# Router logits carried as eight extra columns of a graph layer's products and edge sums

## The chip, the core and the metric

The kernel runs on one NeuronCore of a Trainium2 chip. The metric is the device time of one execution in microseconds (us). All arithmetic is float32.

## What is computed

A graph layer is followed by a mixture of eight experts with two chosen per node. There are 6250 nodes with 256 features and 100000 edges, sorted by destination.

```python
x = x + gnn(layernorm(x))          # agg = segment_sum(h[src], dst) / max(deg, 1)
                                   # concat([h, agg]) @ W.T + b,  W is 256 x 512
x = x + ffn(layernorm(x))
# ffn: layernorm again, * gamma + beta = xn
# logits = xn @ Wr + br            (8 experts)
# top 2, softmax over them = w
# y = sum over e of w[e] * (gelu(xn @ W1[e] + b1[e]) @ W2[e] + b2[e])
```

## The kernel before

**Lead.** W is split into halves. `center_weights` subtracts the column means from each half, which gives `gc`, so that a product with the raw x is the layer norm's product up to the factor 1/deviation. The 49 tiles of 128 nodes are taken in blocks of four (`TB`). For each block `z_block` multiplies the transposed x (`x_t`, loaded in that form) with the second half of `gc` (line 198), ScalarE scales by the reciprocal deviation and writes `zt` (line 226), and SP stores it to `z_d` in DRAM (line 229). Between the products of a block, VectorE computes the statistics of the next one (`z_statistics`, lines 162 and 163) and then its reciprocal deviations (`z_deviations`: a variance, a square root on ScalarE, a reciprocal and a Newton step of four instructions). Loads run four blocks ahead. From the fourth block on one further step is done after every second tile (`steps`, line 393): constants, the turning of the edge lists with a cast to integers (line 274), the first row of every window, and four checks that the destinations do not descend (`compare`, lines 284 and 287).

**Edge stage.** The edges are cut into 56 windows of 14 tiles of 128 edges. For every tile POOL issues an indirect load of 128 rows of `z_d` into one of 16 buffers `xg` (line 527). TensorE multiplies them with a one-hot matrix `hot` of their destinations and accumulates in PSUM (`pS`, line 544); a 257th column of ones counts the degree. A row that two windows share is handed on through DRAM. Beside this `u_stages` computes u = x + b + first half of the product, two node tiles at a time, on the first 50 edge tiles, into `u_d`. At the end of a window x1 = u + sums/degree (`window_x1`, line 581), and its statistics are taken.

**Routing.** After four windows (a group) the second layer norm gives `xn` (line 453). `turn` transposes it on TensorE (line 465) and ScalarE evicts it with gamma and beta (line 466); `route` multiplies it with Wr (line 476), and VectorE computes the ranks (lines 482 to 497), ScalarE the exponentials, VectorE the weights and the slots. `sort_tokens` (line 627) moves the rows to their experts' places by a one-hot product, `copy_runs` (line 742) gathers them by register offsets.

**Experts.** A chunk is 4 or 8 windows (sizes 4, 8, 8, 8, 8, 8, 4, 4, 4). The expert products (lines 758, 773, and for overfull experts 790 to 808) are tasks that are spread over the edge tiles by a rate that comes from a deadline; their rows go to `y_d`. Later POOL gathers each node's two rows (line 856), VectorE adds them (line 863), and SP stores the result.

**What sets the order.** The program order on every engine is written out by hand. The class `Steps` says after how many edge tiles a step of the routing follows a window's end, for example `turn` after 15 and `route` after 20, or 10 and 13 in the last two chunks. After the last edge tile the same counter runs on without gathers.

Of the kernel before, what the change touches and what calls it, by code (L numbers as in the profile page):

```python
# [8 lines left out]
F32 = mybir.dt.float32  # L9
# [8 lines left out]
P = 128  # L18
# [13 lines left out]
def gnn_ffn_kernel(ctx: ExitStack, tc: tile.TileContext, x, x_cols, src, dst, gw_t, gb, gamma, beta,  # L32
# [41 lines left out]
    DA = D + 1  # L74
# [22 lines left out]
    z_d = dram.tile([HR, D], F32, name="z_d")  # L97
    u_d = dram.tile([HR, D], F32, name="u_d")
# [23 lines left out]
    gc = u_pool.tile([P, 2 * KD, D], F32, name="gc", bufs=1)  # L122
    early_pools = ctx.enter_context(ExitStack())
    early = early_pools.enter_context(tc.tile_pool(name="early", bufs=2, side="right"))
    gw_sb = early.tile([P, 2 * KD, D], F32, name="gw_sb", bufs=1)
    for h in (1, 0):
        nc.scalar.dma_start(gw_sb[:, h * KD:(h + 1) * KD, :],
                            gw_t[h * D:(h + 1) * D, :].rearrange("(k p) o -> p k o", p=P))
    order = ctx.enter_context(ExitStack())
# [9 lines left out]
    def constants():  # L139
        nc.vector.tensor_scalar(before, ej, 0.0, None, op0=ALU.is_lt)  # L140
        nc.vector.tensor_copy(cols, coli)
        nc.vector.tensor_copy(lane, lanei)
        nc.vector.tensor_scalar(upper, col, lane, None, op0=ALU.is_gt)
# [40 lines left out]

    def center_weights(h):
        pc = ps.tile([P, D], F32, name="pm")
        for k in range(KD):
            nc.tensor.matmul(pc, ones, gw_sb[:, h * KD + k, :], start=(k == 0), stop=(k == KD - 1))
        for k in range(KD):
            nc.vector.scalar_tensor_tensor(gc[:, h * KD + k, :], pc, -1.0 / D, gw_sb[:, h * KD + k, :],  # L190
                                           op0=ALU.mult, op1=ALU.add)

    def product(t0, n, k0):

        pz = ps.tile([P, 2, D], F32, name="ph")
        for i in range(n):
            for k in range(KD):
                nc.tensor.matmul(pz[:, i, :], x_t[:, t0 + i, k, :], gc[:, k0 + k, :],  # L198
                                 start=(k == 0), stop=(k == KD - 1))
        return pz  # L200

    def z_statistics(t0, some):
        n = min(TB, NT - t0)
        if 0 in some:
            mvs[t0] = small.tile([P, TB, 2], F32, name="mv")
        for i in some:
            if i < n:
                statistics(mvs[t0][:, i, :], xts[t0][:, i, :])

    def z_deviations(t0):  # L210
        n = min(TB, NT - t0)
        a = small.tile([P, TB], F32, name="var_eps")
        nc.vector.tensor_scalar(a[:, :n], mvs[t0][:, :n, 1], EPS, None, op0=ALU.add)
        rsqrt(rstd_x[:, t0:t0 + n], a, root(a, n, TB), n, TB)

    def z_block(t0, between):

        n = min(TB, NT - t0)
        after = t0 + TB
        zt = early.tile([P, TB, D], F32, name="zt", bufs=3)  # L220
        for i in range(0, n, 2):
            m = min(2, n - i)
            pz = product(t0 + i, m, KD)
            for j in range(m):
                t = t0 + i + j
                nc.scalar.activation(zt[:, i + j, :], pz[:, j, :], AF.Identity, scale=rstd_x[:, t:t + 1])
# [3 lines left out]
            if after in blocks:  # L230
                z_statistics(after, range(i, i + 2))
            if between:
                between.pop(0)()
        if after in blocks:
            z_deviations(after)
# [25 lines left out]
    def place_edges(parts, follow):  # L261
# [8 lines left out]
        def turn_edges(f, to, c0):  # L270
# [3 lines left out]
            nc.vector.tensor_copy(to.rearrange("p g c -> p c g")[:, c0:c0 + HC, :], pt)  # L274

        QE = EW // 4
        down = early.tile([W, QE], F32, name="down", bufs=1)

        def compare(i):

            at, n = i * QE, QE if i < 3 else QE - 1
            if i == 0:
                nc.vector.memset(wrong, 0.0)
            nc.vector.tensor_tensor(down[:, :n], fs[0][:, at + 1:at + 1 + n], fs[0][:, at:at + n], op=ALU.is_lt)
            if n < QE:
                nc.vector.tensor_tensor(down[:, n:], follow, fs[0][:, EW - 1:], op=ALU.is_lt)
            nc.vector.reduce_sum(wrong[:W, i:i + 1], down, axis=AX.X)
# [885 lines left out]
```

## Time and profile before

| | us |
|---|---|
| runs (median, lowest, highest of 3) | 1253.08, 1251.77, 1257.36 |
| profiled execution, its own time | 1255.72 |
| its span, first to last instruction | 1253.9 |
| mean granted TensorE clock | 0.948 |

In a line of the profile, L527 is line 527 of the kernel; the engine, the operation and the tiles follow, then the count, the busy time in us, the mean of one in ns, and the idle time of the engine before these instructions with what ended it. PE is TensorE's matmul and PEld its weight load, DVE is VectorE, ACT ScalarE, SPq the queue of SyncE. In the timeline a line starts with start and duration in us; instructions of one kind that follow each other are merged, and the brackets hold the idle time before and what ended it. A float32 matmul is two records.

### The profile page before, as it was taken

How to read it: one execution, taken by the hardware profiler on the slowest of the kernel's cores; microseconds unless marked ns; L12 is line 12 of the kernel's file. 1: busy time of each engine (PE TensorE's matmuls, PEld its weight loads, DVE VectorE, ACT ScalarE, POOL GpSimd, SP SyncE). 2: the span in 40 equal slices, each digit the busy share in tenths (PEclk: the TensorE clock that was granted, in tenths of full speed). 3: DMA queues.
4: the chain of work that ended last, by engine and by line, in shares of the span. 5: the costliest groups of instructions: out<-in, count | busy, mean ns of one | idle time of the engine just before them, and what ended most of it. 6: DMA issues, size and time to landing. Idle time of an engine off the chain costs nothing. (4 is left out here: it accounts for less than half of the span.)

```text
span 1253.9 us, 18359 instructions
## 1 busy us (share of the span) xinstructions
PE 1098.8 (88%) x5114; PEld 907.8 (72%) x5114; DVE 679.0 (54%) x2072; ACT 460.8 (37%) x1183; POOL 865.7 (69%) x911
## 2 busy tenths in 40 slices
PE   7798848687888999899998999899999899999872
PEld 6676736565656888688867887688867787877761
DVE  6765638353664448353754447354743647457541
ACT  3310011622074334733374334632374253533510
POOL 2047777777777777777777777777777777656652
PEclk9899988899898999899998999899999999999886
DMA  9879894554544555455554555555554565566663
GB/s 330 286 249 315 250 369 141 139 139 132 146 138 127 154 147 150 141 144 148 142 160 131 148 146 151 142 140 151 139 158 142 164 170 167 150 188 204 189 213 89
DMA packets 139585, 217.17 MB, mean 173 GB/s; under 512 B 23140, under 2 KB 106927, under 8 KB 139350
## 3 DMA queue, kind: packets, MB, share of 16 engines
q0 software_dynamic: 43104, 117.72, 35.2%
q1 hardware_dynamic: 89430, 89.31, 21.7%
q10 hardware_dynamic: 6944, 8.91, 2.1%
q8 instruction: 43, 0.70, 0.2%
q14 instruction: 64, 0.52, 0.1%
HBM read 162.32 MB, written 53.57 MB: 172 GB/s over the span
## 5 line engine op out<-in xcount | busy, mean ns | idle before, releaser
L527 POOL DMA_INDIRECT xg<-z_d,src_i x784 | 748.4, 955 | 292.6 <-issue 110.6
L544 PE MATMUL pS<-xg,hot 128*128 128x257 f32 x1568 | 428.8, 395 | 43.9 <-DMA xg<-z_d,src_i 29.9
L544 PEld LDWEIGHTS pS<-xg,hot 128*128 128x128 f32 x1568 | 295.0, 196 | 118.0 <-DMA xg<-z_d,src_i 51.5
L758 PE MATMUL ph<-xe,w_sb 128*128 128x256 f32 (+1 forms) x1152 | 223.7, 345 | 29.7 <-ACT xe L742 28.0
L758 PEld LDWEIGHTS ph<-xe,w_sb 128*128 128x128 f32 x1152 | 188.4, 199 | 50.8 <-ACT xe L742 30.4
L773 PE MATMUL py<-w_sb,hid 128*128 128x256 f32 x896 | 216.6, 387 | 7.1 <-DVE rows L777 7.1
L773 PEld LDWEIGHTS py<-w_sb,hid 128*128 128x128 f32 x896 | 172.3, 194 | 33.2 <-DVE rows L777 9.2
L765 ACT ACTIVATE hid<-ph,b_sb 128x256 f32<-128x256 f32 (+1 forms) x288 | 103.1, 426 | 232.5 <-PE ph L758 232.3
L742 ACT ACTIVATE xe<-xs x448 | 139.3, 311 | 60.1 <-ACT xe L742 36.1
L538 DVE TENSOR_TENSOR hot<-cols,rel 128x896 f32<-128x896 f32 x112 | 121.1, 1081 | 36.4 <-PE pS L544 32.4
L856 POOL DMA_INDIRECT xg<-y_d,rows_i x90 | 86.8, 965 | 64.5 <-issue 20.0
L198 PE MATMUL ph<-gc,x_t 128*128 128x256 f32 x392 | 100.8, 412 | 13.6 <-DVE u_t L351 10.5
L198 PEld LDWEIGHTS ph<-gc,x_t 128*128 128x128 f32 x392 | 80.1, 208 | 30.0 <-DVE u_t L351 12.1
L630 ACT ACTIVATE xs<-pm,beta_sb,gamma_sb 128x256 f32<-128x256 f32 x112 | 57.2, 561 | 109.7 <-PE pm L627 109.6
L550 DVE TENSOR_TENSOR pS<-pS,row 1x257 f32<-1x257 f32 x55 | 22.9, 417 | 116.1 <-PE pS L544 90.1
L777 DVE TENSOR_TENSOR rows<-py,b_sb 128x512 f32<-128x512 f32 x56 | 38.5, 688 | 84.5 <-PE py L773 84.5
L554 ACT ACTIVATE sums<-pS 128x257 f32<-128x257 f32 x56 | 21.5, 383 | 170.4 <-DMA xu<-x_dram 58.7
L627 PE MATMUL pm<-to,xn 128*128 128x256 f32 x224 | 59.2, 387 | 10.2 <-DVE rest L659 3.5
L863 DVE SCALAR_TENSOR_TENSOR xg<-xg,w,xg 128x256 f32<-128x256 f32 x90 | 42.8, 483 | 34.4 <-DMA xg<-x_d 22.0
L790 PE MATMUL ph<-w_sb,xe 128*128 x108 | 53.6, 621 | 4.3 <-DVE rows L794 3.3
L808 PE MATMUL py<-w_sb,hid 128*128 x216 | 53.6, 392 | 4.1 <-ACT hid L802 2.5
L627 PEld LDWEIGHTS pm<-to,xn 128*128 128x128 f32 x224 | 42.4, 192 | 19.5 <-issue 10.9
(172 smaller groups left out, 904.2 us busy)
## 6 DMA issues: line engine op xcount, KB each, us to landing
y_d<-rows SPq DMA_DIRECT2D x56, 256.0 KB
xg<-z_d,src_i POOLq DMA_INDIRECT x784, 2.9
w_sb<-w_dram ACTq DMA_DIRECT2D x16, 512.0 KB
x_d<-x SPq DMA_DIRECT2D x56, 128.0 KB
sums_d<-sums SPq DMA_DIRECT2D x55, 128.5 KB
x<-u_d SPq DMA_DIRECT2D x55, 128.0 KB
x_t<-x_cols_dram SPq DMA_DIRECT2D x12, 512.0 KB
xu<-x_dram SPq DMA_DIRECT2D x24, 256.0 KB
```

What stands on the lines that cost most here:

```text
L198: nc.tensor.matmul(pz[:, i, :], x_t[:, t0 + i, k, :], gc[:, k0 + k, :], start=(k == 0), stop=(k == KD - 1))
L527: nc.gpsimd.indirect_dma_start(out=xg[(g * C + c) % XG][:, :D], out_offset=None, in_=z_d[:, :], in_offset=bass.IndirectOffsetOnAxis(ap=src ...
L538: nc.vector.tensor_tensor(hot, col[:, None, :].to_broadcast([P, HC, P]), V.rel[:, c:c + HC, None].to_broadcast([P, HC, P]), op=ALU.is_equal)
L544: nc.tensor.matmul(V.pS, V.hot[c // HC][:, c % HC, :], xg[(V.g * C + c) % XG], start=(c == 0), stop=(c == C - 1))
L627: nc.tensor.matmul(px[:, k, :], G.xn[i][:, k * P:(k + 1) * P], G.one_hot[i], start=True, stop=True)
L630: nc.scalar.activation(xs[:, at:at + 2 * P], px[:, k, :], AF.Identity, bias=beta_sb[:, k:k + 1], scale=gamma_sb[:, k:k + 1])
L742: nc.scalar.activation(K.xe[:, :, bass.ds(v[2 * i], CAP)], src[:, :, bass.ds(src_at, CAP)], AF.Copy)
L758: nc.tensor.matmul(ph[:, i, a * S:(a + 1) * S], w1_sb[:, U.e + a, k, c * P:(c + 1) * P], K.xe[:, k, (U.e + a) * S:(U.e + a + 1) * S], star ...
L765: nc.scalar.activation(U.hid[:, c, a * S:(a + 1) * S], ph[:, i, a * S:(a + 1) * S], AF.Gelu, bias=b1_sb[:, U.e + a, c:c + 1])
L773: nc.tensor.matmul(U.py[:, h, :], U.hid[:, c, h * P:(h + 1) * P], w2_sb[:, U.e + h * UE // 2, c, :], start=(c == 0), stop=(c == KH - 1))
L790: nc.tensor.matmul(ph, K.xe[:, k, at:at + P], w1_sb[:, bass.ds(T.e, 1), k, :].rearrange("p a h -> p (a h)"), start=(k == 0), stop=(k == KD ...
L856: nc.gpsimd.indirect_dma_start(out=V.y2[r], out_offset=None, in_=y_d[K.index][:, :], in_offset=bass.IndirectOffsetOnAxis(ap=G.rows[:, r, i ...
```

## The change

The router's logits are linear in x1 up to mean, deviation and a constant. With wg = gamma * Wr and rc = wg less its column means, the logits are (x1 @ rc) / deviation + (beta @ Wr + br). So x1 @ rc is carried along. W.T @ rc is appended to each half of W.T as eight columns, `z_d`, `u_d`, the edge sums and x1 get 264 columns instead of 256 (the degree's column is then the 265th), and u's product gets eight more columns for x @ rc itself. The transposes, their evictions and the product with Wr are dropped from the routing; four small VectorE instructions per group, one per window, take their place, and the steps behind them move 5 or 7 edge tiles forward.

In the lead, the deviations are computed for groups of 4, 4, 8, 8, 8, 8, 8 and 1 tiles, ahead of the blocks; each node tile's product has a PSUM buffer of its own (two of `ph`, two of `pm`, each with one tile, instead of two of `ph` with two tiles); the casts of the edge lists and of `cols` go to ScalarE; the comparisons become subtractions on POOL with one maximum each on VectorE. The router's small products are added, as are loads of W in its own layout, of b by columns, and the loads of Wr, gamma, beta and br come first.

```diff
+    DZ = D + NX
+    DA = DZ + 1
-    z_d = dram.tile([HR, D], F32, name="z_d")
-    u_d = dram.tile([HR, D], F32, name="u_d")
+    z_d = dram.tile([HR, DZ], F32, name="z_d")
+    u_d = dram.tile([HR, DZ], F32, name="u_d")
...
+    nc.scalar.dma_start(wr_sb, wr.rearrange("(k p) e -> p k e", p=P))
+    nc.scalar.dma_start(gamma_sb, gamma)
     for h in (1, 0):
+        nc.scalar.dma_start(gw_rows[:, :, h * D:(h + 1) * D],
+                            gw[:, h * D:(h + 1) * D].rearrange("(k p) i -> p k i", p=P))
+        nc.scalar.dma_start(gw_sb[:, h * KD:(h + 1) * KD, :D],
                             gw_t[h * D:(h + 1) * D, :].rearrange("(k p) o -> p k o", p=P))
+    nc.scalar.dma_start(gb_p, gb_cols)
+    nc.scalar.dma_start(beta_sb, beta)
+    nc.scalar.dma_start(br_sb, bass.AP(tensor=br.tensor, offset=br.offset, ap=[[0, P], [1, NX]]))
...
+    def router_weights():
+        for k in range(KD):
+            nc.vector.tensor_scalar(wg[:, k, :], wr_sb[:, k, :], gamma_sb[:, k:k + 1], None, op0=ALU.mult)
+        for k in range(KD):
+            nc.tensor.matmul(pr, ones, wg[:, k, :], start=(k == 0), stop=(k == KD - 1))
+        for k in range(KD):
+            nc.vector.scalar_tensor_tensor(rc[:, k, :], pr, -1.0 / D, wg[:, k, :], op0=ALU.mult, op1=ALU.add)
+    def router_columns(h):
+        for i in range(KD):
+            for k in range(KD):
+                nc.tensor.matmul(pr[:, i, :], gw_rows[:, k, h * D + i * P:h * D + (i + 1) * P], rc[:, k, :],
+                                 start=(k == 0), stop=(k == KD - 1))
+        nc.vector.tensor_copy(gw_sb[:, h * KD:(h + 1) * KD, D:], pr)
...
+    def product(t, h):
+        n = DZ if h else DZ + NX
+        pz = ps.tile([P, n], F32, name=("ph", "pm")[t % 2])
+        for k in range(KD):
+            nc.tensor.matmul(pz, x_t[:, t, k, :], gc[:, h * KD + k, :n], start=(k == 0), stop=(k == KD - 1))
...
+    def z_deviations(S):
+        a = small.tile([P, 2 * TB], F32, name="var_eps")
+        nc.vector.tensor_scalar(a[:, :S.n], S.mv[:, :S.n, 1], EPS, None, op0=ALU.add)
+        rsqrt(rstd_x[:, S.first:S.first + S.n], a, root(a, S.n, 2 * TB), S.n, 2 * TB)
...
-            nc.vector.tensor_copy(to.rearrange("p g c -> p c g")[:, c0:c0 + HC, :], pt)
+            nc.scalar.activation(to.rearrange("p g c -> p c g")[:, c0:c0 + HC, :], pt, AF.Copy)
...
+            nc.gpsimd.tensor_tensor(down[:, :n], fs[0][:, at:at + n], fs[0][:, at + 1:at + 1 + n], op=ALU.subtract)
-            nc.vector.tensor_tensor(down[:, :n], fs[0][:, at + 1:at + 1 + n], fs[0][:, at:at + n], op=ALU.is_lt)
-            nc.vector.reduce_sum(wrong[:W, i:i + 1], down, axis=AX.X)
+            nc.vector.reduce_max(wrong[:W, i:i + 1], down, axis=AX.X)
...
+                pu = product(t, 0)
+                nc.vector.tensor_tensor(B.ut[:, i, D:], pu[:, DZ:], gb_r, op=ALU.add)
+                nc.vector.scalar_tensor_tensor(B.ut[:, i, :], pu[:, :DZ], rstd_x[:, t:t + 1], B.ut[:, i, :],
...
-    def turn(G, k):
-        pt = ps.tile([P, TG, P], F32, name="pm")
-        for i in range(G.n):
-            nc.tensor.transpose(pt[:, i, :], G.xn[i][:, k * P:(k + 1) * P], ident)
-        nc.scalar.activation(G.xn_t[:, k, :G.n, :], pt[:, :G.n, :], AF.Identity,
-                             bias=beta_sb[:, k:k + 1], scale=gamma_sb[:, k:k + 1])
+    def logits(G):
+        for i in range(n):
+            nc.vector.scalar_tensor_tensor(lg[:, i, :], G.x1[i][:, D:], G.scale[:, i:i + 1], router_b,
+                                           op0=ALU.mult, op1=ALU.add)
     def route(G, work):
-                nc.tensor.matmul(pl[:, i, :], G.xn_t[:, k, i, :], wr_sb[:, k, :],
-                                 start=(k == 0), stop=(k == KD - 1))
...
-            out=xg[(g * C + c) % XG][:, :D], out_offset=None, in_=z_d[:, :],
+            out=xg[(g * C + c) % XG][:, :DZ], out_offset=None, in_=z_d[:, :],
...
-                self.x1, self.var, self.roots, self.norms, self.turn = 2, 4, 5, 7, 10
-                self.route, self.exps, self.weigh, self.choices, self.count = 13, 15, 16, 17, 19
-                self.hot, self.sort, self.each, self.tiles, self.copied, self.pace = 22, 25, 1, 22, 28, 1
+                self.x1, self.var, self.roots, self.norms = 2, 4, 5, 7
+                self.route, self.exps, self.weigh, self.choices, self.count = 8, 10, 11, 12, 14
+                self.hot, self.sort, self.each, self.tiles, self.copied, self.pace = 17, 20, 1, 17, 23, 1
```

## The prediction

> **What bounds the kernel now.** I read the page's busy shares first, then the gather's group, then the POOL timeline piece by piece, because the shares alone (PE 88%, POOL 69%) point to the wrong engine.
>
> ```profile
> PE 1098.8 (88%) x5114; PEld 907.8 (72%) x5114; DVE 679.0 (54%) x2072; ACT 460.8 (37%) x1183; POOL 865.7 (69%) x911
> L527 POOL DMA_INDIRECT xg<-z_d,src_i x784 | 748.4, 955 | 292.6 <-issue 110.6
> ...
> L476 PEld LDWEIGHTS pm<-wr_sb,xn_t 128*128 128x128 f32 x224 | 28.6, 200 | 7.0 <-ACT xn_t L466 6.3
> L465 PEld LDWEIGHTS pm<-ident,xn 128*128 128x128 f32 x112 | 15.0, 149 | 4.5 <-DVE xn L453 1.2 <-DVE pS L550 0.6
> ```
>
> A gather occupies POOL for 0.946 us (the median), and 0.30 us pass before the next one whatever the reason given. From the first gather to the last, the timeline shows that beat almost unbroken:
>
> ```profile
> 74.99 1.15 POOL L527 DMA_INDIRECT xg<-z_d,src_i  x1 [52.59 <-DVE rel L535]
> ...
> 1084.86 0.94 POOL L527 DMA_INDIRECT xg<-z_d,src_i  x1 [0.30 <-issue]
> ...
> 1087.36 0.95 POOL L527 DMA_INDIRECT xg<-z_d,src_i  x1 [0.30 <-issue]
> ```
>
> Between 75.0 and 1087.4 POOL issues 784 node gathers and some 20 row gathers in 1012.4 us, 1.25 us each; gaps above 0.33 us add only about 1.3 us (0.44, 0.91 and 0.99), instructions longer than 1 us about 7 us. So the span is three pieces: a lead of 75.0 us, an edge stage of 1012.4 us set by POOL, and a tail of 166.5 us.
>
> The lead, by windows (the columns after the stretch are PE, PEld, DVE, ACT, POOL busy, granted clock, DMA share, GB/s):
>
> ```profile
> 20.00:40.00 20.00, 17.18 (x93) 13.46 (x91) 17.32 (x73) 8.06 (x22) 1.89 (x2) 1.00 1.07 392
> 40.00:60.00 20.00, 16.15 (x58) 12.97 (x58) 15.14 (x67) 5.43 (x16) 0.00 (x0) 0.83 0.75 264
> L162 DVE BATCH_NORM_STATS2 st<-xt 128x6 f32<-128x256 f32 x49 | 19.7, 402 | 0.0
> ```
>
> VectorE is full but for its waits on the root (10.8 us in all), and it never waits for a load (idle 0.0 before the statistics). DMA is saturated too from 20 to 45 us, but four blocks ahead of the compute. The tail, by the timeline:
>
> ```profile
> 1112.30 0.60 PE L544 MATMUL pS<-xg,hot 128*128 128x257 f32 x2
> ...
> 1130.96 1.97 PEld L476 LDWEIGHTS pm<-wr_sb,xn_t 128*128 128x128 f32 x16
> ...
> 1178.61 7.33 PEld L758 LDWEIGHTS ph<-xe,w_sb 128*128 128x128 f32 x64
> ...
> 1233.72 0.94 POOL L856 DMA_INDIRECT xg<-y_d,rows_i  x1 [17.24 <-DMA y_d<-rows]
> ```
>
> The last gather goes out at 1087.4, yet PE adds its edges only at 1112.3: PE lags by nearly the ring of 16. The last chunk is routed until 1178.6, its experts run to 1231, and POOL waits 17.24 us for their rows.
>
> **The lead.** Removed from VectorE: 5 of 13 deviation chains (8 groups remain: 4, 4, five of 8, and 1), each 1.4 us from the variance to the last Newton step including the wait for the root, so 7.0 us; four index casts of 0.81 and one of `cols` of 0.42, 3.7 us, which go to ScalarE; four comparisons of 0.59, 2.4 us, which go to POOL before its first gather, when it idles 52.6 us. Added: two products, two subtractions and three small copies for the router, the bias tiles and two copies of rc, about twelve instructions of 0.13 to 0.3 us, 2 us. VectorE's total goes from 26 (49 statistics at 0.53 a pair) + 18.2 + 6.1 + about 7 of other steps = 57 us, which is what the 60.9 us between the first zt (11.40) and the last (72.30) show, to 26 + 11.2 + 7 + 2 = 46.
>
> PE: a weight load and its matmul are one record each; a record at 256 columns comes every 0.216 us. Eight more columns are taken in proportion, 0.223. The z products are 196 such records, 43.7 us, plus turns, centring, router columns and biases, about 6 us; some 3.6 us of it fit into PSUM before the first zt. So PE too needs about 46 us. ScalarE gets five casts of some 0.5 us (the nearest row is zt, 0.47 for 256 elements) on 24 us busy in 75: covered by its waits; behind a cast that waits for its transposes stand the next zt, for well under a microsecond. The comparisons on POOL have a price on VectorE: while POOL cast an index tile, one Newton product took 1.44 us instead of 0.16 (start 18.79). Four such hits would be 5 us, none 0; most VectorE instructions beside that cast kept their time, so I count 1, inside the margin below.
>
> The new wait is at the front. wr, gamma and gw's rows now precede gw_t on ACT's queue: three issues of 0.48 us and 256 KB at 395 GB/s (0.66 us) put its landing from 4.3 to 6.4 us. PE's centring, all z products behind it and VectorE's first statistics behind rc wait for that, so the first zt comes at about 13.5 instead of 11.4.
>
> 13.5 + 46.4 = 60, plus 2.7 from the last zt to the first gather (72.3 to 75.0) is 63, a gain of 12, if nothing interferes. DMA: 21.7 MB moved in the lead, now 0.5 MB of gw rows and 0.2 MB of wider z more, 22.4 MB at 395 GB/s is 57 us, plus about 3 at the start and 4 for the last block: 64. The five small loads that used to run at 86 to 91 us join the saturated stretch too; each has 128 to 256 tiny pieces, and I allow 1 to 3 us. ACT issues seven loads more, before any of its work; SP loses four at 86 to 90 us and otherwise keeps its order. With two limits at 63 to 66 and none of the overlap perfect, I take 67.5: **-7.5 us**, ends 0 and -12.
>
> **A rule against the wider rows.** In 300 to 900 us the DMA view gives the gathers' queue
>
> ```profile
> q0 software_dynamic: 22957, 62.73, 40.0%
> ```
>
> for 479 gathers: 48 packets each and 0.50 us of all 16 engines (40% of 600 us / 479). The Trainium skill, "DMA: Bandwidth & Descriptors", section "How a descriptor splits into AXI transactions", says that reads go in pieces of 256 B from aligned addresses. A 1024-byte row is 4 pieces; one of 1056 bytes starting at a multiple of 32 touches always 5, with 36.5 beats on average against 32. By that rule a gather takes 0.57 to 0.63 us of the engines (estimate), the stage's DMA share goes from 0.53 to about 0.6, and nothing is lost in the edge stage: 1.25 us of POOL covers it. In the lead, z writes of 6.4 MB (16 us at 395 GB/s) would take 2 to 4 us more, and the gain there would be -4. By the row above (bytes alone, +3%) it is -7.5; I keep that, since no compute waits for a load there today, and hold the 3.5 for the range. From 80 to 120 us, where DMA is at 1.00 and 0.93, gathers land later; the ring of 16 (20 us) covers that, and without it up to 5 us would be lost.
>
> **The edge stage.** The gather moves 264 elements instead of 256. No row shows POOL at another width: every gather of this kernel has 1024-byte rows. If POOL's 0.946 us goes by rows (128 in both), it costs nothing; if by bytes, 3.1% is 29.6 ns, times 784 is 23.2 us. It may not fall, as no row or index goes. The equal 946 ns from z_d, u_d and y_d fits work per row, so I take 0, and both ends count below. PE: 1568 records grow by 2.6% (6.7 ns each from 0.216), +10.5 us, and u's 196 records by 16 columns, +2.6; removed are the transposes and logits, 336 records. In the tail one group's take 0.58 + 0.58 + 1.97 us, about 3.1, so 14 groups 44. The net -31 us of PE lies under POOL and is worth nothing before 1087, as are 22 us of ScalarE (xn_t, 28 x 0.78) and VectorE's +9 (u's bias columns, 49 x 0.19) and +8 (56 logits of 0.19 against 14 sums). Stage: **0 us**.
>
> **The tail.** PE reached the ring's full depth only after 950 us. In its last 130 tiles two groups are routed, -6.4, and the edges add 1.7; but routing ends 5 or 7 tiles earlier, so the experts too start earlier and put about 4 us before the last edges (chunk 7's 42 us of tasks over 56 tiles, five tiles more). PE at 1112.3 comes forward only by about 1. Then from 1112.3 to 1178.6, 66 us, PE has 54 us of work: 128 records of L758 (15), 64 of L773 (14), L808 and L790 (15), sort (4), the router (3.1), the rest 3. Of that go 3.1 and the 4 already done; and the last group's logits no longer wait for two transposes, two evictions and 16 records in PE's order: xn is ready at 1124.9, logits came at 1133.06. That is up to 7 us of chain, of which I count 1 beyond PE's share. 1 + 3.1 + 4 + 1 = **-9 us**, ends -3 (the chain is set by the copies, 16 us on ScalarE) and -20 (PE's lag gone entirely). Everything after 1178.6 moves along; POOL has 17 us of slack there.
>
> **Sum.** 75.0 - 7.5, 1012.4 + 0, 166.5 - 9: 1253.9 - 16.5 = 1237.4 of span. The profiled execution took 1255.7 (span and 1.8 around), 2.6 above the median of 1253.1, so the median becomes 1236.6: **1237**.
>
> **Rivals.** (1) The lead doesn't shrink: the later start, the small loads and unaligned writes in a saturated DMA queue eat what VectorE gives back. For it: DMA at 1.07 from 20 to 40 us. Against: no engine waits for a load. 0 - 6 = 1247. (2) POOL pays for width: descriptors or packets are built per byte. One mechanism, L527, 784 times; 21 ns cancel the gain, 29 ns make the kernel slower by over 0.5%. For it: 48 packets of 2.7 KB a gather, so rows are packed four to 4 KB, which 1056 does not fit; a third data packet is closed per engine. Against: equal times from all sources. At 29.6 ns: 1260; at a third more (packets), far above. (3) Both gains whole: the lead at 63, PE without a lag at the end, -12 - 20 = 1221.
>
> **Chances.** About 0.5% (6 us) is what a measurement here can tell from no change. My forecast 0.52, (1) 0.18, (2) 0.20, (3) 0.10. Faster: the first, a third of (1), and (3), 0.66 with what rounding of cases leaves; same 0.15; slower 0.19. The forecast's own range is 1229 to 1244; to leave out at most 2 in 10 it must reach (3) and the near end of (2): 1222 to 1262.
>
> **What would show it.** The gather's median still 946 ns and its first start at 65 to 70 us (right); 975 ns or more (rival 2). VectorE's busy time before the first gather near 42 us; the last edge matmul about 24 us after the last gather; no PE record between xn and the logits; the last chunk's first L758 about 82 us behind the last gather instead of 91. I am wrong if the beat of 1.25 us grows, if gathers wait for PE before 200 us, or if the lead stays at 75.

## The result and the profile after

The changed kernel takes 1251.57 us (median of 20 runs, 1248.30 to 1255.41), the kernel before 1253.92 beside it (20 runs, 1251.77 to 1259.94). The ratio is 0.9976, 95% interval 0.9965 to 0.9988: a gain of 1.5 to 4.4 us where 16.5 were forecast. Its profiled execution took 1251.55 us, with a span of 1249.6. Runs e9 to e12, e17 and e18 were made on chips where the kernel before itself took 1461 and 1472 us; of them only ratios and the lead are used.

The page of the changed kernel, its busy shares, its gather and the gathers' DMA queue:

```profile
PE 1081.8 (87%) x4806; PEld 869.3 (70%) x4806; DVE 684.6 (55%) x2137; ACT 446.0 (36%) x1155; POOL 866.3 (69%) x915
...
q0 software_dynamic: 43104, 120.94, 37.3%
...
L594 POOL DMA_INDIRECT xg<-z_d,src_i x784 | 745.0, 950 | 287.5 <-issue 115.7
```

PE is 17 us less busy, and a gather costs POOL what it did (mean 950 ns against 955). POOL's timeline gives the stages:

```profile
72.42 1.18 POOL L594 DMA_INDIRECT xg<-z_d,src_i  x1 [41.44 <-DMA xu<-x_dram]
...
1061.79 0.94 POOL L594 DMA_INDIRECT xg<-z_d,src_i  x1 [3.09 <-PE pS L611]
...
1087.52 0.95 POOL L594 DMA_INDIRECT xg<-z_d,src_i  x1 [0.30 <-PE pS L611]
```

The gathers' DMA queue from 300 to 900 us, which the prediction showed for the kernel before with 22957 packets and 40.0%:

```profile
q0 software_dynamic: 22994, 64.79, 42.4%
```

The lead went from 75.0 to 72.4 us, the edge stage from 1012.4 to 1015.1, the tail from 166.5 to 162.1. New in the edge stage are waits of POOL for PE like the 3.09 us at 1061.79: the ring of 16 was full. PE in the tail, then POOL's gather of the last expert rows:

```profile
1112.31 0.61 PE L611 MATMUL pS<-xg,hot 128*128 128x265 f32 x2
...
1174.68 5.58 PE L825 MATMUL ph<-xe,w_sb 128*128 128x128 f32 x33 [2.04 <-ACT xe L809]
```

```profile
1229.23 0.94 POOL L923 DMA_INDIRECT xg<-y_d,rows_i  x1 [11.55 <-DMA y_d<-rows]
```

The last edge matmul comes when it did (1112.3), the last chunk's experts 3.9 us earlier and the gather of the last expert rows 4.5.

All kernels on the chips of about 1253 us, each from its one profile (us; the edge stage runs from the first gather's start to the last one's; stalls are POOL's waits over 0.45 us within it, less 0.30 each; the tail is counted from the end of the last edge matmul; median and ratio to before are those of the timed runs):

| kernel | first zt | first gather | edge stage | stalls | tail | median | ratio, 95% interval |
|---|---|---|---|---|---|---|---|
| before | 11.4 | 75.0 | 1012.4 | 1.3 | 141.0 | 1253.92 | |
| changed | 15.8 | 72.4 | 1015.1 | 7.4 | 136.7 | 1251.57 | 0.9976 (0.9965-0.9988) |
| e1 long old | 15.2 | 73.6 | 1014.9 | 4.5 | 140.4 | 1250.78 | 0.9980 (0.9966-0.9994) |
| e2 norms 6 | 15.3 | 72.9 | 1018.2 | 8.4 | 136.8 | 1254.57 | 1.0004 (0.9990-1.0019) |
| e3 wide only | 10.9 | 73.6 | 1011.2 | 1.3 | 140.7 | 1253.39 | 1.0001 (0.9988-1.0013) |
| e4 narrow only | 11.0 | 69.6 | 1013.8 | 2.0 | 141.3 | 1252.30 | 0.9994 (0.9976-1.0012) |
| e5 groups of 4 | 15.2 | 77.7 | 1012.6 | 4.8 | 135.7 | 1254.07 | 1.0010 (0.9993-1.0026) |
| e6 sub on VectorE | 15.2 | 72.8 | 1014.2 | 5.3 | 134.9 | 1249.07 | 0.9970 (0.9959-0.9982) |
| e7 both | 15.2 | 77.1 | 1015.4 | 5.5 | 133.5 | 1254.47 | 1.0015 (0.9999-1.0032) |
| e8 wide, both | 10.9 | 75.2 | 1010.8 | 2.2 | 142.4 | 1258.15 | 1.0030 (1.0010-1.0051) |
| e13 rows only | 11.2 | 73.2 | 1012.1 | 2.6 | 141.5 | 1254.81 | 1.0010 (0.9994-1.0026) |
| e14 penult. old | 15.4 | 71.2 | 1012.1 | 3.3 | 146.0 | 1260.40 | 1.0074 (1.0053-1.0095) |
| e15 tail order | 15.3 | 73.6 | 1014.2 | 5.7 | 138.4 | 1253.41 | 0.9997 (0.9983-1.0011) |
| e16 e14 and e15 | 15.4 | 72.5 | 1013.3 | 4.2 | 142.2 | 1257.36 | 1.0050 (1.0032-1.0069) |

One profile of a stage is good to some 2 us: the seven kernels with the changed lead (changed, e1, e2, e6, e14, e15, e16) have first gathers from 71.2 to 73.6. Groups of rows are therefore compared where there are several.

### The profile page after: what moved, and what is told of

Same layout as the page of the kernel before. It is cut to its first block, busy times and chain, and to the rows that moved or that the text cites. A ratio compares the mean times of both kernels' runs of the same rounds, so it can differ in the third digit from the quotient of the medians.

```text
span 1249.6 us, 17771 instructions
## 1 busy us (share of the span) xinstructions
PE 1081.8 (87%) x4806; PEld 869.3 (70%) x4806; DVE 684.6 (55%) x2137; ACT 446.0 (36%) x1155; POOL 866.3 (69%) x915
## 3 DMA queue, kind: packets, MB, share of 16 engines
q0 software_dynamic: 43104, 120.94, 37.3%
## 5 line engine op out<-in xcount | busy, mean ns | idle before, releaser
L611 PE MATMUL pS<-xg,hot 128*128 128x265 f32 x1568 | 441.9, 404 | 63.1 <-DMA xg<-z_d,src_i 35.7
L825 PE MATMUL ph<-xe,w_sb 128*128 128x256 f32 (+1 forms) x1152 | 226.9, 349 | 23.9 <-ACT xe L809 23.9
L825 PEld LDWEIGHTS ph<-xe,w_sb 128*128 128x128 f32 x1152 | 193.3, 203 | 47.7 <-ACT xe L809 26.8
L840 PE MATMUL py<-w_sb,hid 128*128 128x256 f32 x896 | 213.0, 382 | 4.4 <-DVE rows L844 4.3
L621 ACT ACTIVATE sums<-pS 128x265 f32<-128x265 f32 x56 | 21.7, 388 | 167.8 <-issue 56.4
L617 DVE TENSOR_TENSOR pS<-pS,row 1x265 f32<-1x265 f32 x55 | 23.4, 426 | 92.4 <-PE pS L611 76.7
L256 PE MATMUL ph<-gc,x_t 128*128 128x264 f32 (+1 forms) x200 | 57.5, 413 | 10.5 <-DVE u_t L415 6.3
L857 PE MATMUL ph<-w_sb,xe 128*128 x108 | 56.5, 649 | 7.2 <-DVE rows L861 6.7
```

The lines of the kernel that those rows point to most:

```text
L256: nc.tensor.matmul(pz, x_t[:, t, k, :], gc[:, h * KD + k, :n], start=(k == 0), stop=(k == KD - 1))
L611: nc.tensor.matmul(V.pS, V.hot[c // HC][:, c % HC, :], xg[(V.g * C + c) % XG], start=(c == 0), stop=(c == C - 1))
L825: nc.tensor.matmul(ph[:, i, a * S:(a + 1) * S], w1_sb[:, U.e + a, k, c * P:(c + 1) * P], K.xe[:, k, (U.e + a) * S:(U.e + a + 1) * S], star ...
L840: nc.tensor.matmul(U.py[:, h, :], U.hid[:, c, h * P:(h + 1) * P], w2_sb[:, U.e + h * UE // 2, c, :], start=(c == 0), stop=(c == KH - 1))
L857: nc.tensor.matmul(ph, K.xe[:, k, at:at + P], w1_sb[:, bass.ds(T.e, 1), k, :].rearrange("p a h -> p (a h)"), start=(k == 0), stop=(k == KD ...
```

## The lead: what the width costs

**e3 and e4.** The changed lead with the router taken out of the columns; e4 also drops the columns.

```diff
-    DZ = D + NX
+    NZ = NX                      # e4: NZ = 0
+    DZ = D + NZ
...
+    nc.vector.memset(gw_sb[:, :, D:], 0.0)
...
-    router_weights()
-    router_columns(1)
...                               # turn, route and its steps as before; u rows of 256
```

> The changed kernel's lead and its z rows of 264 columns, but the 8 further columns hold zeros and carry nothing: router_weights, router_columns, the biases and logits are left out, and the router runs as in the kernel before (turn, 32 transposes and 16 small matmuls per group, its steps' distances). u rows have 256 columns. Theory (the lead lost its gain to the serial router chain ahead of the first z product, 15.77 us instead of 11.40): first zt near 11.5 to 12, first gather near 68 to 69 us, edge stage 1012.5, tail 166.5, time 1247 to 1249. Rival (width): PE at 264 columns and 1056-byte rows set the lead's pace and the edge stage suffers from the width, first gather 71 to 72 and edge stage 1015: 1252 to 1254.

> As the kernel with zeros in the 8 further columns, but without these columns: rows of 256 everywhere, so only the lead's other part is left (deviations of eight tiles at once, casts moved to ScalarE and POOL, subtractions on POOL, loads and steps reordered, z products tile by tile). Theory: the width costs the lead 52 tiles x 3% of 0.89 us = 1.4 us and the edge stage nothing: first gather 1 to 2 us ahead of the wide kernel's, edge stage 1012.5 in both, time 1246 to 1248. Rival (width costs the edge stage and the pace of the lead): 4 us or more between the two kernels.

First zt came 4.9 us earlier in e3 than in the changed kernel, and the last one later (69.6 against 68.9). So the serial router chain ahead of the first product, which I took for the thief, does not move the lead's end: my theory fell at once. What moved it was the width, 73.6 against 69.6. The edge stage was not longer for it (1011.2 and 1013.8). Both missed their forecast times: 1253.39 and 1252.30 us cannot be told from the kernel before, so e4's shorter lead is seen in its profile alone.

**e13 and e9.** Is it PE's 264 columns, the rows' length, or where they start? e13 is e3 with 264 columns only in zt, z_d, gathers and sums; e9 is e4 with each row 32 bytes off.

```diff
 # e13, against e3
-        n = DZ if h else D
+        n = D
+        nc.scalar.activation(zt[:, :, D:], ones[...], AF.Copy)
 # e9, against e4
-    z_d = dram.tile([HR, DZ], F32, name="z_d")
+    z_flat = dram.tile([1, HR * D + 64], F32, name="z_flat")
+    z_d = z_flat[0:1, 8:8 + HR * D].rearrange("a (r d) -> (a r) d", d=D)
```

> The wide kernel with the width in the rows alone: z_d, zt, the gathers and the edge sums keep 264 columns (the last 8 hold ones that nothing reads; a small copy on ScalarE fills them in each block of zt), but gc, the z products and the centring have 256 again. The shift of the narrow rows by 32 bytes left the first gather at 69.00 (69.6 unshifted, 73.6 wide), so it isn't where rows start. Theory (a row of 1056 bytes costs the transfers more than its 3% of bytes): first gather 72 to 74 us and 370 to 385 GB/s at full share. Rival (PE's 264 columns cost the lead): 69 to 70.5 us and 390 GB/s or more.

> The narrow kernel (rows of 256 everywhere, no router in the columns) with z_d shifted by 8 elements in DRAM, so that each row of 1024 bytes starts 32 bytes behind a multiple of 1024; nothing else changes. The wide kernel (1056-byte rows) ended its lead 4.0 us behind the narrow one (first gather 73.6 against 69.6). Theory (where a row starts costs it: the Trainium skill, DMA: Bandwidth & Descriptors, the section on AXI transactions): the rate at full share falls from 396 to 370 or 380 GB/s and the first gather goes to 72 to 74 us. Rival (the further bytes and PE's 264 columns): 69.5 to 70.5 us and 390 GB/s or more, as in the narrow kernel. The edge stage: 1012 to 1014 us by both, since POOL's 0.946 us per gather didn't move with 1056-byte rows.

POOL's first gather and the window of 30 to 55 us (its last two columns are DMA share and GB/s) in e4, narrow:

```profile
69.59 1.18 POOL L559 DMA_INDIRECT xg<-z_d,src_i  x1 [39.83 <-DMA xu<-x_dram]
```

```profile
30.00:55.00 25.00, 23.91 (x122) 18.84 (x121) 18.91 (x84) 14.10 (x30) 0.00 (x0) 1.00 1.07 395
```

in e9, narrow but shifted:

```profile
69.00 1.18 POOL L561 DMA_INDIRECT xg<-z_flat,src_i  x1 [39.99 <-DMA xu<-x_dram]
```

```profile
30.00:55.00 25.00, 24.06 (x124) 19.23 (x123) 19.06 (x86) 13.82 (x30) 0.00 (x0) 1.00 1.07 387
```

in e13, long rows with PE at 256 columns:

```profile
73.16 1.18 POOL L558 DMA_INDIRECT xg<-z_d,src_i  x1 [44.18 <-DMA xu<-x_dram]
```

```profile
30.00:55.00 25.00, 25.00 (x121) 20.35 (x121) 17.30 (x79) 14.63 (x36) 0.00 (x0) 0.92 1.07 377
```

and in the changed kernel:

```profile
30.00:55.00 25.00, 25.00 (x131) 20.22 (x132) 18.51 (x89) 14.49 (x32) 0.98 (x2) 1.00 1.07 371
```

At one and the same DMA share of 1.07 the transfers moved 395 GB/s in e4, 387 in e9, 377 in e13 and 371 in the changed kernel. e13 shows that the wider rows cost the lead its 4 us and PE's 264 columns do not (73.6 and 73.2 against 69.6 and 69.0); e9 that the shift costs no time. The lower rate is only a part of the 4 us. From 30 to 55 us the changed kernel moved 0.6 MB less than e4, which is 1.5 us. e3 and e13 had moved 7.4 MB by 30 us and e4 8.0, so that over a third of their loss stood before that stretch; why is not settled.

The prediction had two numbers for these rows. As a cost in time, the split of the Trainium skill ("DMA: Bandwidth & Descriptors", "How a descriptor splits into AXI transactions") gave 2 to 4 us for the z writes, which is about the size that was found, and 0.57 to 0.63 us of the engines for a gather. The gathers do not bear it out: the line of queue 0 above gives 42.4% of 600 us / 479 = 0.53 us (0.52 in e6, 0.50 in the kernel before), hardly more than the 0.52 of the bytes alone. e9 does not decide. Counted in pieces its rows should cost as much as the wide ones (five); counted in the section's beats, by my estimate, they need 33 instead of 32, and its rate was 2% lower. That the skill's estimate met the lead's loss is therefore luck in part.

**e5 to e8.** In the changed kernel PE stood still for 3.25 us at 26 to 29: a group of eight needs eight statistics ahead of its first zt, and POOL's work held VectorE's Newton steps.

```diff
 # e5, e7, e8: groups of four
-        S.first, S.n, S.mv = t0, min(TB if t0 < 2 * TB else 2 * TB, NT - t0), None
+        S.first, S.n, S.mv = t0, min(TB, NT - t0), None
 # e6, e7, e8: in descents, ahead of its maximum
-            nc.gpsimd.tensor_tensor(down[:, :n], ..., op=ALU.subtract)
+            nc.vector.tensor_tensor(down[:, :n], ..., op=ALU.subtract)
```

> The changed kernel with the deviations of four tiles at a time throughout (min(TB, ...) in place of min(TB if t0 < 2 * TB else 2 * TB, ...)). Theory A (the group of eight makes PE wait at 26 to 29 us, since its eight statistics and its Newton steps stand ahead of the first zt of the group): the group of four is ready some 2 us earlier, the wait of 3.98 us on ScalarE shrinks to 1 to 2, first gather 70 to 71 us. Rival (the DMA engines at 1.07 from 25 to 60 us set the lead's end): first gather stays at 72 to 73. Either way under 0.2% of the time.

> The changed kernel with the four subtractions of the edge check on VectorE, each just ahead of its maximum, instead of on POOL. Theory B (POOL's subtractions, 27.38 to 30.98 us, hold VectorE's Newton steps: 1.62, 0.88 and 0.85 us instead of 0.16 each): these steps fall back to 0.17 where no cast runs beside them, the first zt of the first group of eight comes about 2 us earlier than 29.32, first gather 70 to 71 us. Rival (DMA engines): 72 to 73 us, and VectorE has 4 x 0.5 us more to do.

> Groups of four and the subtractions on VectorE together. Theories A and B together: the stall of PE (3.25 us before 29.85) is gone, first gather 69 to 70 us, time 1247 to 1249 us. Rival (DMA engines): PE waits for x_t or z_d buffers instead, and the first gather stays at 72 to 73, 1251 to 1252 us.

> The kernel with zeros in the 8 further columns (no router chain ahead of z, router as before) with both edits: groups of four, subtractions on VectorE. In its first form it started z 4.9 us before the changed kernel and ended it 0.7 us later, with VectorE waiting for loads of x (3.70 us at 28 us) and ScalarE for a zt buffer (5.63 us at 31.9). Theory (the eight-tile group held z's rows back, and SP's queue with them the loads that stand behind): without it z keeps its lead, first gather 67 to 69 us instead of 73.6. Rival (the transfers themselves set the end: 1056-byte rows, share 1.07): first gather 72 to 74 as before.

One Newton step on VectorE, in the changed kernel beside POOL's work and in e6 with POOL idle:

```profile
25.81 1.62 DVE L170 TENSOR_TENSOR newton<-newton,var_eps 128x8 f32<-128x8 f32 x1
```

```profile
24.85 0.17 DVE L170 TENSOR_TENSOR newton<-newton,var_eps 128x8 f32<-128x8 f32 x1
```

The stall was POOL's doing, but the theory named the wrong instruction for the longest hit. The step of 1.62 us ran beside POOL's cast of an index list (25.74 to 27.41 us), which e6 has too, but there it began at 25.30 us, as the last of these steps ran. The next two, 0.88 and 0.85 us, ran beside the subtractions. Each ended 0.02 to 0.03 us after the POOL instruction beside it. Ending the stall was worth nothing: e6's first gather is at 72.78. PE's waits for zt fell from 3.3 to 2.1 us, and VectorE now waited 3.6 us for loads of x instead: the transfers were the limit. The groups of four were a clear miss, 77.7 and 77.1. VectorE's waits for the root, in the changed kernel and in e5 (total, times, longest):

```profile
DVE rstd_x L167 <- ACT root L162: 6.4, 8, 2.3
```

```profile
DVE rstd_x L167 <- ACT root L162: 8.0, 13, 1.8
```

Five more chains, each with its wait and its small steps, cost 4 to 5 us (e5 and e7), but only 1.6 in e8 against e3. So the groups of eight earn up to 5 of the 7 us that the prediction gave them, and the rows take 4 back.

**e17.** z writes on ScalarE's queue, so that loads need not stand behind them (with e6's edit):

```diff
-                nc.sync.dma_start(rows_of(z_d, ...), zt[:, i0:i + m, :])
+                nc.scalar.dma_start(rows_of(z_d, ...), zt[:, i0:i + m, :])
```

> The changed kernel with the subtractions on VectorE and the writes of z_d issued on ScalarE's queue. In the changed kernel each load of x stands on SP's queue behind the z write of the block before (SP waited 20 us for zt in the lead, and the transfers moved only 281 and 193 GB/s from 15 to 25 us). Theory (SP's order starves the transfers): the loads run ahead, the holes at 15 to 25 us fill, first gather 69.5 to 71 us instead of 72.4 to 72.8, time 1247 to 1249. Rival (1056-byte rows at the full share set the lead's end, the order of the queue doesn't): 72 to 73.5 us, 1249 to 1251.

A miss: the first gather came at 78.94, against 73.95 for the changed kernel on that chip (e18). SP's queue in e17 stood still from 29.6 to 37.8 us:

```profile
29.10 0.50 SPq L446 DMA_DIRECT2D x_t<-x_cols_dram  x1
37.81 0.38 SPq L193 DMA_DIRECT2D xt<-x_dram  x1
```

The loads did not run ahead but waited, by the profile for z writes (12.6 us in all), and the transfers moved 99 GB/s from 25 to 30 us and 163 from 35 to 40. Why a load waits for them is not settled. But later in the same lead, with these writes on a queue of their own, the stream was as fast as in e4, rows of 1056 bytes and all (a 1056-byte packet took 47 ns there, 51 in the changed kernel):

```profile
50.00:55.00 5.00, 5.00 (x27) 4.04 (x26) 4.58 (x25) 3.45 (x7) 0.00 (x0) 1.00 1.06 392
55.00:60.00 5.00, 5.00 (x23) 3.98 (x22) 3.63 (x16) 2.30 (x7) 0.00 (x0) 1.00 1.07 398
```

e18, with the writes on SP's queue, ran at 367 GB/s from 30 to 45 us on the same chip. So, by this one profile, the length of the rows does not lower the rate by itself; the rate was lower where they shared SP's queue with the loads. What happens there is open.

## The edge stage: the price of earlier steps

**e1, e10 and e14.** Steps of before put back: for the long chunks (e1), or for the last chunk but one (e10 and e14, one edit).

```diff
 # e1
-                self.route, self.exps, self.weigh, self.choices, self.count = 12, 15, 17, 18, 22
-                self.hot, self.sort, self.each, self.tiles, self.copied, self.pace = 25, 29, 2, 27, 37, 1.5
+                self.route, self.exps, self.weigh, self.choices, self.count = 20, 22, 24, 25, 29
+                self.hot, self.sort, self.each, self.tiles, self.copied, self.pace = 32, 36, 2, 34, 44, 1.5
 # e10, e14
+            if index == len(chunks) - 2:
+                self.route, self.exps, self.weigh, self.choices, self.count = 13, 15, 16, 17, 19
+                self.hot, self.sort, self.tiles, self.copied = 22, 25, 22, 28
```

> The changed kernel with the long chunks' steps put back to the distances of before (route 20, exps 22, ... copied 44); the last two chunks keep the new, shorter ones. Theory (route's block on VectorE): with norms and logits at step 11 and route at 12, VectorE runs 6.6 us without a break and PE's evictions wait, which ended in 7.1 us of ring stalls on POOL between 1038 and 1065 us; apart again, the last edge gather starts about 1012.5 us behind the first instead of 1015.1, the wait of 6.1 us before L857 at 1033 is gone, and the time is 1247 to 1249 us. Rival (the wider rows, 265 columns in the edge matmul and 6% more bytes, cost the edge stage): the stalls stay, 1251 to 1252 us.

> The changed kernel with the steps of before for the last chunk but one alone, from route on (route 13, exps 15, ..., copied 28), norms and logits staying at 7. Theory (norms, logits and route in one block of 6.6 us on VectorE held the eviction L861, and PE 6.12 us before L857 at 1033.9; POOL's ring then stalled 5 times from 1038 to 1065, 6.7 us): the block is split, PE's wait there falls under 3.5 us, the late stalls to 2 to 3 us, the last gather comes 3 to 4 us earlier. That chunk's experts start 5 steps later, which can cost the tail up to 3 us. Time 1247.5 to 1251. Rival (the stalls come from the experts' work itself): stalls as now, 1251 to 1253.

> The same edit as in e10_penult_old, since on that chip the kernel before took 1461 us and its edge stage was not bound as here. Expected as there: PE's wait of 6.12 us before L857 near 1034 falls under 3.5 us, the late stalls of POOL from 6.7 to 2 to 3 us, the last gather comes 3 to 4 us earlier, the tail 0 to 3 us longer, time 1247.5 to 1251; by the rival (the experts' work itself) the stalls stay and the time is 1251 to 1253.

(The step numbers that the first text gives are those of the long chunks; the block of 6.6 us belongs to the last chunk but one, with norms at 7 and route at 8.) The steps that meet, on VectorE in the changed kernel, are 6.6 us from the reciprocal at 1026.55 to the eviction at 1033.16. PE before one product of a further expert tile, in the changed kernel and in e14:

```profile
1033.89 3.78 PE L857 MATMUL ph<-w_sb,xe 128*128 x4 [6.12 <-DVE rows L861]
```

```profile
1033.42 1.99 PE L857 MATMUL ph<-w_sb,xe 128*128 x4 [1.47 <-DVE rows L861]
```

With route five tiles behind norms, VectorE gets to the eviction in between; PE's wait falls from 6.12 to 1.47 us, POOL's stalls behind 1000 us from 6.7 to 2.4 (whole waits), and the last gather comes 4.1 us earlier (1083.4; 1.2 of it from the lead). In e1 that product didn't wait at all, since the experts of the chunk ahead stand elsewhere, and the late stalls were 2.2 us. So the late stalls are the change's own: the steps that it moved forward run into each other on VectorE. They are not the width's: e3, e8 and e13 have the wide rows and 1.3 to 2.6 us. e1's edge stage stayed at 1014.9 us all the same, not the 1012.5 expected, with six stalls at 124 to 145 us (2.9 us). Stalls at that place are in e2, e7, e14 and e15 too and hardly in the changed kernel and e6; no run explains them.

The expectation for the tail was wrong. The same five steps cost e14 9.3 us there (146.0 against 136.7): the last chunk's first copy came 53.0 us behind the last edge matmul instead of 45.4, presumably because the experts of the chunk ahead now run into its routing. The time was 1260.40 us. e1 paid 3.7 us and broke even. e10's ratio, 0.9938 (0.9913 to 0.9964), lies behind the changed kernel's 0.9877 in e18, but the intervals touch and the chips differ. The earlier steps cost these stalls and are worth more in the tail.

## The tail: where nine became six

In the changed kernel the last group's root is there at 1120.97, but VectorE takes it up at 1126.66, behind combines that wait for gathered rows, and behind an eviction. ScalarE, then VectorE:

```profile
1120.77 0.20 ACT L162 ACTIVATE root<-var_eps 128x4 f32<-128x4 f32 x1
```

```profile
1124.75 0.48 DVE L930 SCALAR_TENSOR_TENSOR xg<-xg,w,xg 128x256 f32<-128x256 f32 x1 [2.31 <-DMA xg<-y_d,rows_i]
1125.15 0.68 DVE L844 TENSOR_TENSOR rows<-py,b_sb 128x512 f32<-128x512 f32 x1
...
1126.66 0.17 DVE L167 RECIPROCAL rstd<-root 128x4 f32<-128x4 f32 x1
```

In the kernel before the same reciprocal waited for nothing but the root:

```profile
1122.48 0.18 DVE L152 RECIPROCAL rstd<-root 128x4 f32<-128x4 f32 x1 [0.94 <-ACT root L147]
...
1133.29 0.19 DVE L482 TENSOR_REDUCE top<-lg 128x4 f32<-128x32 f32 x1
```

In the changed kernel that maximum ran at 1129.83. From the reciprocal to it the change saves 7.6 us (10.8 to 3.2), and 4.2 of that had gone by the time the chain began.

**e2, e11, e15, e12, e16.**

```diff
 # e2, in the last two chunks: every step from norms on one earlier
-                self.x1, self.var, self.roots, self.norms = 2, 4, 5, 7
-                self.route, self.exps, self.weigh, self.choices, self.count = 8, 10, 11, 12, 14
+                self.x1, self.var, self.roots, self.norms = 2, 4, 5, 6
+                self.route, self.exps, self.weigh, self.choices, self.count = 7, 9, 10, 11, 13
...
 # e11, e15: the same in the last chunk only, e6's edit, and
-            nc.sync.dma_start(y_d[K.index][at:at + P, :], ys[:, 0, :])
+            nc.scalar.dma_start(y_d[K.index][at:at + P, :], ys[:, 0, :])
 # e12, e16: these and the edit of e14
```

> The changed kernel with norms, logits and all that follows them one step earlier in the last two chunks (norms 6, route 7, exps 9, ..., copied 22), so that the last group's reciprocal stands on VectorE right behind its variances and ahead of six combines and one eviction of 128x512. Theory (the tail lost its gain in VectorE's order): the root is there at 1120.97 us but the reciprocal started at 1126.66; it now starts near 1121.2, the exp comes 4 to 5 us earlier than 1130.3, and the time falls by 3 to 5 us, to 1247 to 1249. Rival (the expert products on PE and the combines on VectorE fill the tail whatever the order): what is moved ahead is paid back before the last chunk's copies, which start at 1158 as now; 1251 to 1252 us.

> The changed kernel with the subtractions on VectorE, norms and all behind them one step earlier in the last chunk only, and the writes of the extra experts' rows to y_d (in three) issued on ScalarE's queue instead of SP's. With norms earlier in the last two chunks the last eviction came 2.7 us sooner behind the last edge matmul (109.7 instead of 112.4), but the gather of its rows not (116.6 against 116.3): the write waited on SP's queue behind stores of finished rows (L908, 4.04 us). Theory (SP's queue gave the gain back): the gather follows the eviction by 2.5 us as before, last edge matmul to end 131.5 to 133.5 us instead of 136.7, time 1245 to 1247. Rival (the transfers themselves take that long at this time): 3.9 to 6.9 us of landing stay, 1248 to 1250.

> The same edits as in e11_tail_order, for the same reason. Theory (SP's queue gave the gain of the earlier routing back): the gather of the last rows follows the last eviction by 2.5 us instead of 3.9, last edge matmul to end 131.5 to 133.5 us instead of 136.7, time 1245 to 1247. Rival (the transfers take that long at this time): 1248 to 1250.

> The edits of the tail (subtractions on VectorE, norms one step earlier in the last chunk, y_d writes on ScalarE's queue) and of the last chunk but one (its steps from route on as before) together. If both theories hold and do not collide: edge stage 1011 to 1012, last edge matmul to end 132 to 134 us, time 1243 to 1246. If the later experts of the last chunk but one run into the last chunk's routing: tail 136 to 139 us, 1248 to 1250.

> The same edits as in e12_tail_and_penult, for the same reason. If both theories hold and do not collide: edge stage 1011 to 1012 us, last edge matmul to end 132 to 134, time 1243 to 1246. If the later experts of the last chunk but one run into the last chunk's routing: 136 to 139, 1248 to 1250.

In e2 the reciprocal came 8.1 us behind the last edge matmul instead of 13.7, the copies 42.6 instead of 45.4, the last eviction 109.7 instead of 112.4; and the gather of its rows 116.6 instead of 116.3. Its last writes on SP's queue:

```profile
1224.65 4.04 SPq L908 DMA_DIRECT2D out_dram<-xg  x2
1228.79 1.71 SPq L882 DMA_DIRECT2D y_d<-rows  x2
```

They stood behind stores of finished rows. e15, whose reciprocal came 9.2 us behind the last edge matmul, takes them off that queue, and they did not get through sooner. ScalarE's queue, the tile's landing times, and POOL's gather:

```profile
1223.94 2.90 ACTq L880 DMA_DIRECT2D y_d<-rows  x2
```

```profile
DMA to landing us min/median/max: 2.6/2.9/4.4
```

```profile
1231.26 0.94 POOL L921 DMA_INDIRECT xg<-y_d,rows_i  x1 [12.83 <-DMA xg<-x_d]
```

The gather followed the last eviction by 4.8 us (before 2.5, changed 3.9, e2 6.9), so SP's queue alone is not the cause; that theory fell. e15's last eviction came no sooner either (113.6 us behind the last edge matmul). So in e2 and e15 the earlier start of the chain shortened the tail by nothing. What makes these last writes slower is open; POOL's line names the loads of x1 rows issued just ahead. e2 also had the longest edge stage (1018.2, 5.0 us of stall at 1062), as earlier steps should. e16 shows e14's cost in the tail again, but smaller: 142.2 us against e15's 138.4, and 1257.36 against 1253.41 us on the same chip. e11 has no gain (1.0008, 0.9977 to 1.0038). e12, which adds e14's edit to it, is not slower (0.9975, 0.9938 to 1.0011) and does not show that cost.

**e18**, the changed kernel once more:

> The changed kernel once more, on the same chip. One profile of it against one of before gave lead -2.6, edge stage +2.7, tail from the last edge matmul -4.3 us; a repeat shows how much of that is one execution's chance. If these are the change's own, first gather 71.5 to 73.5, late stalls at the same places with 5 to 7 us in sum, last edge matmul to end 134 to 137; ratio 0.9965 to 0.9988. If chance makes up half of it, single stages differ by over 2 us from the first profile.

Its chip told nothing of the edge stage: a gather took 954 ns on average, but from 100 to 1080 us POOL alone had 65 us of waits that the profile puts down to "remote", of which the profiles of the changed kernel, e1 and e6 show none, and PE was busy for 79% of the span. Its first gather, 73.95, lies just above the 71.5 to 73.5 expected. The ratio was 0.9877 (0.9830 to 0.9924), a gain of 1.2%, larger than the expected one; why is open. For the repeat of the stages e5, e6 and e7 stand in: they share the changed kernel's steps, and the stalls of 0.9, 3.1 and 1.0 us at 1057 to 1070 recur in each.

No kernel beat the changed one beyond doubt: e6 has 0.9970 (0.9959 to 0.9982), which overlaps its 0.9976.

## Why the prediction was wrong

- **POOL per row (rival 2 did not come true): right.** The gather keeps its median of 946 ns, and 43104 packets move 120.94 MB instead of 117.72 in as many packets. There is no third data packet: those of four rows grew from 4096 to 4224 bytes.
- **The lead, -7.5: wrong; -2.6 in the profile, 72.7 as the mean of seven (-2.3).** The step that failed is the choice between row and rule: "by the row above (bytes alone, +3%) it is -7.5; I keep that". The mis-sized term is the width: the wider rows cost 4.1 us where their bytes alone were counted. Without them the lead came to 69.0 and 69.6, near the 67.5. "No compute waits for a load there today" was true and no argument: with less for VectorE to do, the transfers were next. They were also taken to run at 395 GB/s almost throughout. In the changed kernel they moved 281 and 193 GB/s from 15 to 20 and 20 to 25 us, which is 1.6 MB or 4 us less, and 371 at the full share. VectorE's term was nearly sound: its busy time before the first gather and its waits for the root fell by 9 us together (51.3 + 10.8 to 46.7 + 6.4) of the 11 forecast. The "new wait at the front" was too small (first zt 15.8, not 13.5) and without effect (e3).
- **The edge stage, 0: wrong, +2.7.** Kernels with the changed steps (changed, e5, e6, e7) have 1014.3 on average, those with the steps of before (before, e3, e4, e8, e13) 1012.1: +2.2, though single ones overlap. The prediction moved "experts 4 us earlier" and asked nothing of what then meets on VectorE: the wait added, PE behind an eviction behind norms, logits and route, was not in the list. The excess of long instructions fell, the stalls rose from 1.9 to 5.8 us.
- **The tail, -9: right in its way, but a third of it did not come.** From the last edge matmul on, the same groups give 141.4 and 135.2, so -6.2; the one profile shows -4.3. "PE at 1112.3 comes forward by about 1" was wrong (0). The chain's 7 us existed (7.6), and 4.2 of them went to the reciprocal's place behind the combines; but taking that place back gained nothing (e2, e15), so which other term was too large stays open. The last chunk's first expert product came 87 us behind the last gather, not the 82 forecast (91 before).
- **Rival 1 was the closest**, with 1247 and half of its reason: longer rows in a saturated DMA queue. It lacked the edge stage's loss.
- **The sum.** The two profiles give -2.6 + 2.7 - 4.3, or -4.2. The profiled execution of before stood 1.8 us above the median of its 20 runs and that of the changed kernel at its median, so -2.4 remains, as measured (1253.92 to 1251.57). By the groups it would be -6.3, or -4.5 after the same 1.8, just past the far end of the measured -1.5 to -4.4.

## To carry to other kernels

When a stage is limited by one engine and the transfers run at their full share beside it, cost the change against the transfers too, with a rate that was measured for the new rows in the same queue, not against the bytes: 8 columns more ate most of what VectorE gave. Steps moved forward in a hand-ordered schedule bring other steps together; look for the eviction that then stands behind a block on VectorE and for the ring it fills. And before giving up such a step for its stall, price what it bought at the end: here five tiles of the last routing but one were worth 4 to 9 us of tail (e16 and e14) and cost 1 to 3 of the edge stage.

## What the runs showed of the hardware

- With z rows of 1056 bytes on SP's queue beside the loads, the lead's transfers ran at 371 to 382 GB/s, with rows of 1024 at 395 (e4), all at a DMA share of 1.07. With the 1056-byte rows on ScalarE's queue they ran at 392 and 398 (e17). A start 32 bytes off cost 2% of the rate (387 in e9).
- A gather of 128 rows costs POOL 946 ns for 1024- and 1056-byte rows alike, and 48 packets. Of the 16 DMA engines it takes 0.50 and 0.52 to 0.53 us.
- A VectorE product of 128x8, 0.17 us by itself, took 1.62 beside a POOL cast of 56x1792, and a multiply and add 0.88 beside a POOL subtraction of 56x448; each ended with the POOL instruction. The statistics of 128x256 kept their 0.40 us beside the subtractions.
